# Attention's output through memory to feature rows: the division in two side steps, the projection without transposes

## The chip, the cores and the metric

The kernel runs on one core of a Trainium2 chip. A core has five engines that run side by side, each through its own instructions in order: TensorE (PE, matrix products, with its weight loads shown as PEld), VectorE (DVE), ScalarE (ACT), GpSimd (POOL) and SyncE (SP). Matrix products are written to PSUM, a small memory of banks; all else is held in SBUF, both with 128 partitions. Transfers between SBUF and the device's memory (DRAM) are issued by an engine's queue, mostly SP's here, and are moved by 16 DMA engines. An instruction that waits holds back all that stand behind it on its engine.

The metric is the device time of one execution in microseconds (us), the median of several runs.

## The reference

Two attentions and two MLPs on x of shape [2048, 256], in float32:

```
x = x + attn_a(layernorm(x))     # 16 query heads, 4 key/value heads, rotary angles, biases
x = x + ffn(layernorm(x))        # weights of 4 bits with scales, 2048 features, gelu(gate) * up
x = x + attn_b(layernorm(x))     # 16 heads, no biases
x = x + ffn(layernorm(x))        # the same weights again

# each attention, head size 16, causal:
scores = einsum('bthd,bshd->bhts', q, k) * 16 ** -0.5
probs  = softmax(where(causal, scores, -inf))
out    = einsum('bhts,bshd->bthd', probs, v).reshape(B, S, 256) @ Wo.T
```

## The kernel before

**Tiles.** The 2048 rows are four blocks of 512 (TB), block b in `xt[b]` as 128 partitions x 4 x 256. The 16 heads are four groups g of four. An attention is 16 *units* (b, g): 512 queries of one block against all keys up to them, for four heads. A unit has three parts.

- *Maxima* (`max_steps`): scores with queries on the partitions (L658, masks by L633 on the diagonal), and the maximum over the keys on DVE (L670, `mx`). `gather` brings the maxima together on DVE (L682 to L692), `turn` turns them on PE (L699) and ACT copies them to `mT` (L705).
- *Values* (`value_steps`): 4(b+1) key tiles, two `pair` steps each. PE subtracts the maximum (L747) and adds the scores with keys on the partitions (L752), ACT takes the exponential (L764, `e`), and PE multiplies by the values (L732) into `ps_av`. Each head has 32 partitions of `ps_av`: rows 0 to 15 are the output's features, row 16 (HD) is the sum of the exponentials, by a column of ones in the values.
- *The end* (`end`): ACT copies `ps_av` to `o` in SBUF (L779).

**From `o` to x.** `divide` transposes `o` in four 128x128 pieces on PE (L786), takes the reciprocal of the sums on DVE (L791) and multiplies into `att[b]` (L794), which has queries on the partitions and all 256 features along them. When the block's four groups are done, `out_steps` makes two halves of it: `turn` transposes `att` back to features on the partitions (L814, four a half) and ACT copies them to `aT` (L819); `project` multiplies by Wo (L826) and DVE adds to `xt[b]` (L831).

**The order.** All engines' orders are written by hand. In `run`, the value steps of unit n are the main list. Its side list holds the maxima of unit n+1 (8 steps per block of keys, and `gather`) and, spread among them by `blend`: the preparation of the next block (units with g = 0 and 1), the unpacking of the MLP's weights (first attention, from unit 4 on), and the `out_steps` of the block before (units with g = 0). `weave` runs, after each main step, as many side steps as are due, so that all are done two main steps ahead of the end. `divide` of the unit before stands first in the side list, so it comes after the first pair:

```
side = late + (blend(steps, more) if steps else more)
steps, end, divide = self.value_steps(b, g)
weave(steps, side, rest=2)
```

What is left of the last unit goes to the following MLP's first block, as side steps of its 16 `features` steps.

**Buffers and queues.** `ps_s` has three PSUM buffers, shared by the scores of both kinds and by the MLP; `ps_m` (transposes, projections, preparation) and `ps_av` have one each. SP issues nearly all transfers, in the order written: eight loads of queries `qT` for unit n+2 at the start of unit n (L619, three buffers), the stores of q and k as a high and a low part (L540, L544), the packed weights (L318), and the MLP's down weights `wd` (L907). POOL's queue loads `kT` (L606).

**The names that matter below:** L658/L670 scores and maxima, L747/L752/L764/L732 values, L779 `o`, L786/L791/L794 `divide`, L814/L819 `turn`, L826/L831 `project`, L619 `qT`.

Of the kernel before, what the change touches and what calls it, by code (L numbers as in the profile page):

```python
# [8 lines left out]
F32 = mybir.dt.float32  # L9
# [58 lines left out]
def tile_hybrid_layers(  # L68
# [326 lines left out]
    class Attention:  # L395
# [317 lines left out]
        def value_steps(self, b, g):  # L713

            nk = NT * (b + 1)
            held = {"pending": []}

            def values(half):

                self.settle()  # L720
                kt, q0, es_ = held["pending"][0]
                few = TB - q0 <= TB // 2
                if half == 1:
                    held["pending"].pop(0)
                    if few:
                        return
                elif kt == 0:
                    held["av"] = ps_av()
                own = slice(q0, TB) if few else slice(*((q0, TB // 2), (TB // 2, TB))[half])
                for j in range(4):  # L730
                    h = g if self.first else 4 * g + j
                    nc.tensor.matmul(  # L732
                        held["av"][32 * j : 32 * j + 32, own],
                        lhsT=self.vv[kt // NT][:, kt % NT, h * VW : h * VW + 32],
                        rhs=es_[j // 2][:, j % 2, own],
                        start=(kt == 0 and half == 0), stop=(kt == nk - 1),
                    )

            def pair(kt, p):
                q0 = max(0, kt - NT * b) * P  # L740
                diagonal = kt >= NT * b
                keys = slice((kt % NT) * P, (kt % NT + 1) * P)
                self.settle()
                pt = ps_s()

                for r in range(2):
                    nc.tensor.matmul(  # L747
                        pt[:, r, q0:], lhsT=sel[64 * r : 64 * r + 64, p, :],
                        rhs=self.mT[b, g][64 * r : 64 * r + 64, q0:], start=True, stop=False,
                    )  # L750
                for r in range(2):
                    nc.tensor.matmul(  # L752
                        pt[:, r, q0:], lhsT=self.key_rows(kt // NT, g, p, r, keys),
                        rhs=self.qT[b, g][64 * r : 64 * r + 64, p, q0:],
                        start=False, stop=not diagonal,
                    )
                e = self.wk.tile([P, 2, TB], F32, tag="e", name="e", bufs=4)

                def masked():
                    self.add_mask(pt, 1, q0)  # L760
                    exponentials()

                def exponentials():
                    nc.scalar.activation(e[:, :, q0:], pt[:, :, q0:], AF.Exp, scale=QK_SCALE)  # L764

                if diagonal:
                    self.owed.append(("exp", masked))
                else:
                    exponentials()
                if p == 0:  # L770
                    held["es"] = [e]
                else:
                    held["pending"].append((kt, q0, held["es"] + [e]))

            def end():
                values(0)
                values(1)
                o = pre.tile([P, TB], F32, tag="o", name="o")
                nc.scalar.copy(o, held["av"])  # L779
                held["o"] = o  # L780

            def divide():
                o = held["o"]
                pt = ps_m()
                for i in range(NT):
                    nc.tensor.transpose(  # L786
                        pt[:, i * P : (i + 1) * P], o[:, i * P : (i + 1) * P], ident
                    )
                heads = pt.rearrange("p (t j c) -> p t j c", t=NT, c=32)
                rec = small.tile([P, NT, 4], F32, tag="rec", name="rec")  # L790
                nc.vector.reciprocal(rec, heads[:, :, :, HD])  # L791
                if g == 0:
                    self.att[b] = pre.tile([P, NT, NG, 4, HD], F32, tag="att", name="att")
                nc.vector.tensor_tensor(  # L794
                    self.att[b][:, :, g], heads[:, :, :, :HD],
                    rec.unsqueeze(3).broadcast_to([P, NT, 4, HD]), ALU.mult,
                )

            steps = []
            for kt in range(nk):  # L800
                for p in range(2):
                    scored = lambda kt=kt, p=p: pair(kt, p)
                    steps.append((scored, lambda p=p: values(p)) if kt else scored)
            return steps, end, divide

        def out_steps(self, b):
            held = {}

            def turn(n):
                pt = ps_m()  # L810
                for i in range(2):
                    flat = self.att[b][:, 2 * n + i].rearrange("p g j c -> p (g j c)")
                    for c in range(2):
                        nc.tensor.transpose(  # L814
                            pt[:, (2 * i + c) * P : (2 * i + c + 1) * P],
                            flat[:, c * P : (c + 1) * P], ident,
                        )
                aT = pre.tile([P, 2, 2, P], F32, tag="aT", name="aT")
                nc.scalar.copy(aT, pt.rearrange("p (i c t) -> p i c t", i=2, c=2))  # L819
                held[n] = aT  # L820

            def project(n):
                po = ps_m()
                for i in range(2):
                    for c in range(2):
                        nc.tensor.matmul(  # L826
                            po[:, i * D : (i + 1) * D], lhsT=held[n][:, i, c, :],
                            rhs=self.wo[:, c, :], start=(c == 0), stop=(c == 1),
                        )
                to = xt[b][:, 2 * n : 2 * n + 2, :]  # L830
                nc.vector.tensor_tensor(  # L831
                    to, po.rearrange("p (i d) -> p i d", i=2), to, ALU.add
                )

            return [lambda n=n, f=f: f(n) for n in range(2) for f in (turn, project)]

        def run(self, extra, beside):

# [3 lines left out]
            late, ahead = [], []  # L842
            for n, (b, g) in enumerate(units):
                more = []
                if g == 0 and b > 0:
                    more += self.out_steps(b - 1)
                if g == 0 and b + 1 < NB:
                    ahead = self.prep_steps(b + 1)
                    few = -(-len(ahead) // 2)
# [8 lines left out]
                    steps, turn = self.max_steps(*units[n + 1])  # L858
                else:
                    more += beside  # L860
                side = late + (blend(steps, more) if steps else more)
                steps, end, divide = self.value_steps(b, g)
                weave(steps, side, rest=2)
                if turn:
                    turn()
                end()
                late = [divide]
            return late + [lambda: None] * 2 + self.out_steps(NB - 1)


    class Mlp:
# [183 lines left out]
```

## Time and profile before

The median is 1904.03 us of 3 runs (1902.41 to 1907.81). The profiled execution took 1904.93 us, its span from first to last instruction is 1903.1 us.

| | us | of the span |
|---|---|---|
| PE busy | 1772.5 | 93% |
| DVE busy | 1121.3 | 59% |
| ACT busy | 812.9 | 43% |
| POOL busy | 239.0 | 13% |
| L764, exponentials (ACT) | 573.4 | |
| L670, maxima (DVE) | 656.8 | |
| L786, transposes of `o` (PE) | 21.3 | |
| L814, transposes of `att` (PE) | 10.2 | |
| L826, projection (PE) | 31.7 | |
| L779, copies of `o` (ACT), 32 | 18.8 | |
| L819, copies `aT` (ACT), 16 | 9.2 | |
| DMA, mean rate | 34 GB/s | |

The first attention fills the stretch from about 71 to 651 us, the first MLP to 1028 us, the second attention to 1558 us, the second MLP the rest. Units of the second attention last from 12.3 us, (0,2), to 51.5 us, (3,0), counted from one copy of `o` to the next.

How to read the lines that follow: a group is line, engine, operation, what is written <- what is read, partitions x elements, count | busy us, mean ns of one | idle time of the engine just before, and who ended it. A timeline line is start in us, length in us, engine, line, operation, count, and in brackets the idle time before it. A wait line is who waited <- for whom: total us, times, longest us. A line of a stretch is from:to, length, then busy us and count of PE, PEld, DVE, ACT and POOL, the granted clock of PE, DMA's busy share and GB/s. DMA lines end with the median us from issue to landing.

### The profile page before, as it was taken

How to read it: one execution, taken by the hardware profiler on the slowest of the kernel's cores; microseconds unless marked ns; L12 is line 12 of the kernel's file. 1: busy time of each engine (PE TensorE's matmuls, PEld its weight loads, DVE VectorE, ACT ScalarE, POOL GpSimd, SP SyncE). 2: the span in 40 equal slices, each digit the busy share in tenths (PEclk: the TensorE clock that was granted, in tenths of full speed). 3: DMA queues.
4: the chain of work that ended last, by engine and by line, in shares of the span. 5: the costliest groups of instructions: out<-in, count | busy, mean ns of one | idle time of the engine just before them, and what ended most of it. 6: DMA issues, size and time to landing. Idle time of an engine off the chain costs nothing. (4 is left out here: it accounts for less than half of the span.)

```text
span 1903.1 us, 31836 instructions
## 1 busy us (share of the span) xinstructions
PE 1772.5 (93%) x13452; PEld 930.8 (49%) x13452; DVE 1121.3 (59%) x1676; ACT 812.9 (43%) x1069; POOL 239.0 (13%) x437
## 2 busy tenths in 40 slices
PE   5788889998999999999998899999899999999999
PEld 3344444344444446566555444444444444756656
DVE  4466587678788153535345667767877715363442
ACT  1334345465666631312223455555566663131221
POOL 4211311310010010111212010010000001011110
PEclk8879899999999999999999899999999999999999
DMA  4511310310101100000403241050000010000000
GB/s 105 118 46 34 73 26 26 72 41 24 34 24 35 45 6 1 0 1 20 102 1 80 56 83 41 12 95 19 23 7 7 2 46 1 11 1 11 7 6 12
DMA packets 42271, 64.24 MB, mean 34 GB/s; under 512 B 13840, under 2 KB 20880, under 8 KB 41872
## 3 DMA queue, kind: packets, MB, share of 16 engines
q1 hardware_dynamic: 33488, 45.93, 8.3%
q0 software_dynamic: 7680, 15.74, 5.0%
q8 instruction: 106, 1.74, 0.4%
q10 hardware_dynamic: 960, 0.52, 0.1%
q14 instruction: 37, 0.30, 0.1%
HBM read 44.24 MB, written 17.83 MB: 33 GB/s over the span
## 5 line engine op out<-in xcount | busy, mean ns | idle before, releaser
L764 ACT ACTIVATE e<-ps_s 128x1024 f32<-128x1024 f32 (+3 forms) x640 | 573.4, 897 | 433.7 <-PE ps_s L752 216.5
L670 DVE TENSOR_REDUCE mx<-ps_s 128x2 f32<-128x1024 f32 (+3 forms) x640 | 656.8, 1060 | 160.9 <-PE ps_s L633 93.2
L732 PE MATMUL ps_av<-e,v 128*32 128x256 f32 (+1 forms) x4608 | 370.6, 386 | 0.7 <-ACT e L764 0.7
L752 PE MATMUL ps_s<-qT,kT 64*128 64x512 f32 (+3 forms) x1280 | 341.9, 527 | 0.0
L658 PE MATMUL ps_s<-kT,qT 64*128 64x512 f32 (+3 forms) x1280 | 268.6, 428 | 45.4 <-DVE mx L670 20.1
L747 PE MATMUL ps_s<-mT,sel 64*128 64x512 bf16 (+3 forms) x1280 | 232.6, 357 | 36.7 <-DVE mx L670 21.4
L915 PE MATMUL ps_s<-xnT,wg 128*128 128x512 f32 x512 | 240.8, 593 | 0.0
L915 PE MATMUL ps_s<-xnT,wu 128*128 128x512 f32 x512 | 240.6, 592 | 0.0
L747 PEld LDWEIGHTS <-sel 64*128 64x128 bf16 x1280 | 77.1, 93 | 275.8 <-issue 269.4
L658 PEld LDWEIGHTS ps_s<-kT,qT 64*128 64x128 f32 x1280 | 125.7, 191 | 150.9 <-ACT e L764 66.9
L923 DVE TENSOR_TENSOR t<-ps_s,t 128x512 f32<-128x512 f32 x128 | 88.1, 689 | 166.4 <-POOL t L922 164.5
L921 ACT ACTIVATE t<-ps_s 128x512 f32<-128x512 f32 x128 | 76.2, 596 | 246.7 <-PE ps_s L915 246.3
L924 ACT ACTIVATE t<-t 128x512 f32<-128x512 f32 x128 | 80.6, 629 | 201.0 <-DVE t L923 201.0
L915 PEld LDWEIGHTS ps_s<-xnT,wu 128*128 128x128 f32 x512 | 97.3, 190 | 122.5 <-issue 122.5
L922 POOL TENSOR_SCALAR t<-t 128x512 f32<-128x512 f32 x128 | 79.3, 620 | 571.1 <-ACT t L921 570.6
L732 PEld LDWEIGHTS ps_av<-e,v 128*32 128x32 f32 x4608 | 97.0, 109 | 102.8 <-issue 79.8
L915 PEld LDWEIGHTS ps_s<-xnT,wg 128*128 128x128 f32 x512 | 95.3, 190 | 105.2 <-issue 103.5
L925 DVE SCALAR_TENSOR_TENSOR t<-t,ps_s 128x512 f32<-128x512 f32 x128 | 88.0, 688 | 89.0 <-ACT t L924 89.0
L752 PEld LDWEIGHTS ps_s<-qT,kT 64*128 64x128 f32 x1280 | 130.4, 198 | 0.0
L940 PE MATMUL ps_m<-wd,inter 128*128 128x256 f32 x512 | 114.5, 380 | 0.0
L940 PE MATMUL ps_av<-wd,inter 128*128 128x256 f32 x512 | 114.5, 380 | 0.0
L633 PE MATMUL ps_s<-mask_t,mask_w 64*128 64x64 bf16 x2048 | 108.4, 199 | 0.0
(125 smaller groups left out, 1171.5 us busy)
## 6 DMA issues: line engine op xcount, KB each, us to landing
qT<-h SPq DMA_DIRECT2D x256, 64.0 KB, 2.2
kT<-h POOLq DMA_DIRECT2D x96, 128.0 KB, 5.7
h<-high SPq DMA_DIRECT2D x24, 256.0 KB, 3.3
h<-low SPq DMA_DIRECT2D x24, 256.0 KB, 3.0
wd<-wd_kept SPq DMA_DIRECT2D x2, 2048.0 KB, 7.8
wd_kept<-dq_d SPq DMA_DIRECT2D x4, 512.0 KB, 2.7
out<-x SPq DMA_DIRECT2D x16, 128.0 KB, 1.7
x<-x SPq DMA_DIRECT2D x3, 512.0 KB, 5.2
```

What stands on the lines that cost most here:

```text
L633: nc.tensor.matmul(pt[:, r, to], lhsT=mask_w[rows, kind, part, :], rhs=mask_t[rows, kind, part, :], start=False, stop=(part == 1),)
L658: nc.tensor.matmul(pt[:, r, :w], lhsT=self.qT[b, g][64 * r : 64 * r + 64, p, i * P : (i + 1) * P], rhs=self.key_rows(c, g, p, r, slice(0, w)),
L670: nc.vector.tensor_reduce(held["mx"][:, i, 2 * p : 2 * p + 2, c], pt[:, :, :w], AX.X, ALU.max)
L732: nc.tensor.matmul(held["av"][32 * j : 32 * j + 32, own], lhsT=self.vv[kt // NT][:, kt % NT, h * VW : h * VW + 32], rhs=es_[j // 2][:, j % ...
L747: nc.tensor.matmul(pt[:, r, q0:], lhsT=sel[64 * r : 64 * r + 64, p, :], rhs=self.mT[b, g][64 * r : 64 * r + 64, q0:], start=True, stop=False,)
L752: nc.tensor.matmul(pt[:, r, q0:], lhsT=self.key_rows(kt // NT, g, p, r, keys), rhs=self.qT[b, g][64 * r : 64 * r + 64, p, q0:], start=Fals ...
L764: nc.scalar.activation(e[:, :, q0:], pt[:, :, q0:], AF.Exp, scale=QK_SCALE)
L915: nc.tensor.matmul(pt[:, k, :], lhsT=w[:, c, fc * P : (fc + 1) * P], rhs=self.xnT[b][:, c, :], start=(c == 0), stop=(c == 1),)
L923: nc.vector.tensor_tensor(t, gate, t, ALU.mult)
L924: nc.scalar.activation(t, t, AF.Tanh, scale=GELU_C)
L925: nc.vector.scalar_tensor_tensor(t, t, 1.0, gate, ALU.add, ALU.mult)
L940: nc.tensor.matmul(po[:, :D], lhsT=inter[:, fc, i * P : (i + 1) * P], rhs=wd[:, fc, :], start=(fc == 0), stop=(fc == NFC - 1),)
```

## The change

- `end` copies `ps_av` to `o` as before, then stores all of `o` to memory (`o_kept`, 256 KB). From there SP loads the four rows of sums into half of `den` ([128, 32]: four heads x 512 queries spread over 64 partitions), and the 64 feature rows into half of `att` (now [128 features, 512 queries]; two units, g even and odd, fill one). Three transfers a unit.
- After odd g there are two steps. `invert`: DVE takes the reciprocal of `den` (128x32), SP stores it (`rec_kept`) and loads it back with each head's row repeated over 16 partitions (`factor`, 128x512). `divide`: DVE multiplies `att` by `factor` in place, both in SBUF.
- `att` has features on the partitions already, so `out_steps` has no `turn`: `project` reads `att` as its weights.
- `late` isn't first in the side list any more: with part = length // (b + 1), `invert` is put at part // 2, `divide` at part + 1, and after g = 3 the two `project` at part + 4 and part + 6. Behind the last unit, pauses of three empty steps stand before `invert`, before `divide` and before the first `project`.

```diff
 def end():
     values(0)
     values(1)
     o = pre.tile([P, TB], F32, tag="o", name="o")
     nc.scalar.copy(o, held["av"])
-    held["o"] = o
+    kept = dram.tile([4, 32, TB], F32, tag="o", name="o_kept", bufs=2)
+    nc.sync.dma_start(out=kept.rearrange("j c t -> (j c) t"), in_=o)
+    if g % 2 == 0:
+        self.att[b, g // 2] = (
+            pre.tile([P, TB], F32, tag="att", name="att", bufs=2),
+            small.tile([P, 32], F32, tag="den", name="den"),
+        )
+    att, den = self.att[b, g // 2]
+    rows = slice(64 * (g % 2), 64 * (g % 2) + 64)
+    nc.sync.dma_start(
+        out=den[rows], in_=kept[:, HD].rearrange("j (s q) -> j s q", q=32)
+    )
+    nc.sync.dma_start(out=att[rows], in_=kept[:, :HD])
+
+def invert():
+    den = self.att[b, g // 2][1]
+    rec = small.tile([P, 32], F32, tag="rec", name="rec")
+    nc.vector.reciprocal(rec, den)
+    kept = dram.tile([8, TB], F32, tag="rec", name="rec_kept", bufs=2)
+    nc.sync.dma_start(
+        out=kept.rearrange("h (s q) -> (h s) q", q=32), in_=rec
+    )
+    factor = pre.tile([P, TB], F32, tag="factor", name="factor")
+    nc.sync.dma_start(
+        out=factor, in_=kept.unsqueeze(1).broadcast_to([8, HD, TB])
+    )
+    held["factor"] = factor
 
 def divide():
-    o = held["o"]
-    pt = ps_m()
-    for i in range(NT):
-        nc.tensor.transpose(
-            pt[:, i * P : (i + 1) * P], o[:, i * P : (i + 1) * P], ident
-        )
-    heads = pt.rearrange("p (t j c) -> p t j c", t=NT, c=32)
-    rec = small.tile([P, NT, 4], F32, tag="rec", name="rec")
-    nc.vector.reciprocal(rec, heads[:, :, :, HD])
-    if g == 0:
-        self.att[b] = pre.tile([P, NT, NG, 4, HD], F32, tag="att", name="att")
-    nc.vector.tensor_tensor(
-        self.att[b][:, :, g], heads[:, :, :, :HD],
-        rec.unsqueeze(3).broadcast_to([P, NT, 4, HD]), ALU.mult,
-    )
+    att = self.att[b, g // 2][0]
+    nc.vector.tensor_tensor(att, att, held["factor"], ALU.mult)
...
-            return steps, end, divide
+            return steps, end, [invert, divide] if g % 2 else []
 
 def out_steps(self, b):
-    held = {}
-    def turn(n):
-        pt = ps_m()
-        for i in range(2):
-            flat = self.att[b][:, 2 * n + i].rearrange("p g j c -> p (g j c)")
-            for c in range(2):
-                nc.tensor.transpose(
-                    pt[:, (2 * i + c) * P : (2 * i + c + 1) * P],
-                    flat[:, c * P : (c + 1) * P], ident,
-                )
-        aT = pre.tile([P, 2, 2, P], F32, tag="aT", name="aT")
-        nc.scalar.copy(aT, pt.rearrange("p (i c t) -> p i c t", i=2, c=2))
-        held[n] = aT
     def project(n):
         po = ps_m()
         for i in range(2):
+            t = (2 * n + i) * P
             for c in range(2):
                 nc.tensor.matmul(
-                    po[:, i * D : (i + 1) * D], lhsT=held[n][:, i, c, :],
+                    po[:, i * D : (i + 1) * D], lhsT=self.att[b, c][0][:, t : t + P],
                     rhs=self.wo[:, c, :], start=(c == 0), stop=(c == 1),
                 )
...
-    return [lambda n=n, f=f: f(n) for n in range(2) for f in (turn, project)]
+    return [lambda n=n: project(n) for n in range(2)]
 
 def run(self, extra, beside):
...
-        if g == 0 and b > 0:
-            more += self.out_steps(b - 1)
...
-        side = late + (blend(steps, more) if steps else more)
-        steps, end, divide = self.value_steps(b, g)
+        side = blend(steps, more) if steps else more
+        part = len(side) // (b + 1)
+        for at, step in zip((part // 2, part + 1, part + 4, part + 6), late):
+            side.insert(at, step)
+        steps, end, late = self.value_steps(b, g)
         weave(steps, side, rest=2)
         if turn:
             turn()
         end()
-        late = [divide]
-    return late + [lambda: None] * 2 + self.out_steps(NB - 1)
+        if g == NG - 1:
+            late += self.out_steps(b)
+    pause = [lambda: None] * 3
+    return pause + late[:1] + pause + late[1:2] + pause + late[2:]
```

## The prediction

> **What bounds the kernel now.** I read the busy table first, then the same counts by stage, the groups by form, TensorE's waits, the timeline of one unit boundary, and last the DMA issues. All is from one profiled execution: span 1903.1 us, 1904.93 us with what lies around it, 0.9 us above the median of 1904.03; I make the sum against it and subtract from the median.
>
> ```profile
> span 1903.1 us, 31836 instructions
> ...
> PE 1772.5 (93%) x13452; PEld 930.8 (49%) x13452; DVE 1121.3 (59%) x1676; ACT 812.9 (43%) x1069; POOL 239.0 (13%) x437
> ```
>
> ```profile
> 71.00:651.00 580.00, 525.17 (x5385) 248.38 (x5385) 398.51 (x583) 310.12 (x369) 92.29 (x160) 0.96 0.16 40
> 1052.00:1558.00 506.00, 475.24 (x5150) 227.22 (x5148) 349.12 (x442) 301.95 (x358) 19.36 (x35) 0.99 0.14 35
> ```
>
> These two stretches are the attentions (busy PE, PEld, DVE, ACT, POOL; clock; DMA share). PE is busy 91 and 94%, DVE 69%: PE sets the pace, DVE comes next, and DMA (0.14 to 0.16) is nearly free. What is removed or kept, on PE and then DVE:
>
> ```profile
> L826 PE MATMUL ps_m<-wo,aT 128*128 128x256 f32 x128 | 31.7, 390 | 7.4 <-ACT aT L819 7.3
> L786 PE MATMUL ps_m<-ident,o 128*128 128x128 f32 x128 | 21.3, 290 | 0.0
> L814 PE MATMUL ps_m<-ident,att 128*128 128x128 f32 x64 | 10.2, 281 | 3.1 <-DVE att L794 2.7 <-DVE x L831 0.4
> ```
>
> ```profile
> L794 DVE TENSOR_TENSOR att<-ps_m,rec 128x256 f32<-128x256 f32 x32 | 13.6, 424 | 1.1
> L791 DVE RECIPROCAL rec<-ps_m 128x16 f32<-128x16 f32 x32 | 8.2, 257 | 86.6 <-PE ps_m L786 86.6
> ```
>
> The last number is idle time before. DVE's 86.6 us hurts only as far as PE waits for DVE afterwards:
>
> ```profile
> PE ps_s L747 <- DVE mx L670: 21.4, 37, 1.2
> PE ps_s L658 <- DVE mx L670: 20.1, 44, 1.0
> ```
>
> One boundary, into unit (2,2) of the second attention, PE and then DVE; the copy of o (L779) ends at 1298.24, the zero T of my times below:
>
> ```profile
> 1298.29 0.65 PE L786 MATMUL ps_m<-ident,o 128*128 128x128 f32 x4
> 1298.87 0.50 PE L658 MATMUL ps_s<-kT,qT 64*128 64x512 f32 x2
> ...
> 1300.88 0.39 PE L747 MATMUL ps_s<-mT,sel 64*128 64x512 bf16 x2 [0.81 <-DVE mx L670]
> ```
>
> ```profile
> 1299.61 5.28 DVE L670 TENSOR_REDUCE mx<-ps_s 128x2 f32<-128x1024 f32 x5
> 1305.92 2.93 DVE L670 TENSOR_REDUCE mx<-ps_s 128x2 f32<-128x256 f32 x3 [1.02 <-PE ps_s L633]
> ```
>
> ```profile
> qT<-h SPq DMA_DIRECT2D x256, 64.0 KB, 2.2
> h<-high SPq DMA_DIRECT2D x24, 256.0 KB, 3.3
> wd_kept<-dq_d SPq DMA_DIRECT2D x4, 512.0 KB, 2.7
> out<-x SPq DMA_DIRECT2D x16, 128.0 KB, 1.7
> dq_s<-gate_s POOLq DMA_DIRECT2D x32, 32.0 KB, 2.1
> dq_q<-up_p SPq DMA_DIRECT2D x4, 256.0 KB, 3.1
> ```
>
> Last column: us from issue to landing. A chain of four such landings is what the change puts in place of the transposes.
>
> **Part 1, removed.** (a) 32 quartets of L786. By the timeline the next PE work starts 0.58 us after each (1298.29 to 1298.87); in the MLP, where two of them lie, I read 0.44. So 30 x 0.58 + 2 x 0.44 = 18.3 us of PE. Behind it DVE's reciprocal and product (0.68) delay the first maximum by about 0.2, which PE pays at 1300.88: up to 30 x 0.2 = 6 us more. (b) 16 quartets of L814: 12 x 0.55 + 4 x 0.44 = 8.4, plus PE's waits around them: 3.1 before L814, 7.3 for the ACT copy aT, 1.3 where a projection waits for ps_m behind att: 11.7. (c) 16 aT copies on ACT (9.2 us) and 21.8 us on DVE: no direct gain, ACT is idle half the time. Sum 38.4; bounds 27 (18.3 + 8.4, were every wait to return elsewhere) and 44. I take 40, near the top, since both waits vanish with their producers.
>
> **Part 2, added: when the steps become ready.** At each of 32 ends SP waits for the copy of o and issues o_kept, den, att; every second unit adds a reciprocal, rec_kept, factor and one product. 128 issues on SP, 0.46 apart (the eight qT issues take 3.66 us). SP mostly waits, so issue time costs nothing itself; order does. o_kept stands ahead of the eight qT loads of the unit after next. From T: o_kept lands at 2.8 (2.7 taken, between out<-x 1.7 and h<-high 3.3); den, 2.1 as the small load dq_s, at 5.0 (bounds 3.9 to 5.9); att is issued at 3.4, the qT loads until 7.6. Only then rec_kept: 2.0, landing at 9.7; then factor, 2.9 (wd_kept 2.7, dq_q 3.1), at 12.7 (bounds 11.8 to 13.5). In (3,2) no qT is loaded and factor is there at 10.9. The qT loads end 5.5 us later than now, and are first read a unit later; the shortest unit, (0,2), lasts 12.3 us against a landing at 9.8. Without that cover PE would lose the difference four times. The h stores behind them come 2 us later, with two high buffers and later units as cover. The 2 MB load of wd comes after the last att, 38 us or more before its first reader. POOL's queue is not passed.
>
> **Part 3, what waits.** By the new list of side steps, reciprocal stands behind 3 to 4 maxima and product behind 8. In (2,2) above the fourth maximum ends at T + 6.2 and the eighth at 1308.85, T + 10.6; both come 0.7 earlier without the transposes. So reciprocal finds den there (5.5 against 5.0), and product, at 9.9, waits 2.8 for factor. I placed the other units by the same count.
> - Reciprocal: (0,2) and (1,2) and (3,2) arrive at 4.0 to 4.9, the rest at 5 or later; waits add up to 3 us (bounds 0 and 11: den at 5.9 in ten units).
> - Product: arrivals in (1,2), (2,2), (3,0), (3,2) are 11.1, 10.9, 11.9, 9.3 in layer 1 and 9.4, 9.9, 10.9, 10.3 in layer 2: waits of 1.6, 1.8, 0.8, 1.6, 3.3, 2.8, 1.8, 0.6. The product itself is 0.69 (the 128x512 two-input rows). Queued behind it is the next maximum, whose ps_s buffer PE needs two allocations later; by the rows that leaves about 0.8, and DVE idles 2.1 to 2.7 there in three layer-1 units. Wait + 0.69 - 0.8 - idle gives PE losses of 0, 1.7, 0, 0, 2.5, 2.5, 1.7, 0.5: 9 us (bounds 2 and 24). In (0,2) only the next unit's maxima are behind it. In (1,0) and (2,0) it arrives at 15.6 or later; in the MLP at about 16.
> - First projection: three steps behind product, now with a wait on DVE: 1.8, 0.3, 1.2, 0.6, 0.8 in five units, 5 us (0 to 8).
> Costs 17; bounds 2 and 43. DVE's own work is unchanged within 6 us (21.8 out; 16 x 0.96 in).
>
> Sum: 1904 - 40 + 17 = 1881.
>
> One rule speaks against the change beyond this. The Trainium skill, "DMA: Bandwidth & Descriptors", section "Why a DMA increments its semaphore by 16 and not by 1", says a transfer uses only as many of the 16 engines as divide the outermost dimension on both sides: 4 for den and att, 8 for factor. No DMA of this trace has so small an outer dimension. With the page's 436 GB/s for 16 engines I estimate factor at 3.2 us rather than 2.9; by that the sum would be 1883.
>
> **The rivals.**
> - *All hidden.* The landings take the lower bounds and DVE's earlier start pays: 44 - 2 saved, 1862. For it: 0.14 DMA share; against it: rec_kept stands behind eight qT issues.
> - *Not on the path.* The 81 waits of PE on maxima (41.5 us) show that the ps_s loop with DVE sets the pace in part. If quartets' 26.7 us return as such waits, 40 - 27 - 17 leaves 1908, and half of it 1894; I put this case at 1901. Against it: PE 94% busy, and the boundary stall follows the scores, which move up.
> - *DVE held by the round trip (slower).* Place: reciprocal and product in the ten units with g = 2 or (3,0). Each us more on every landing brings den 2 us later and factor about 1 more beyond that: 3 us x 10 = 30 us. Break-even is 23/30 = 0.8 us per landing; at 1.5 more (the loads of down_p take 4.7, those of kT 5.7) the time is 1881 + 45 = 1926. For it: DVE runs in order and a full maximum takes 1.22 of each 1.45 us step, so a held DVE can hardly catch up. Against it: the queue is quiet after boundaries, and 64 KB loads land in 2.2.
>
> **Numbers.** Main case 0.53 (1866 to 1898 for itself), all hidden 0.16, not on the path 0.14, DVE held 0.17. A measurement here tells 0.3%, 5.7 us. Faster 0.53 + 0.16 + 0.05 of the third = 0.74; same 0.08; slower 0.18 with a tail of the third. Range: 1858 (44 saved, the rest the run-to-run spread) to 1911 (38 saved, 43 paid, short of the far slow tail).
>
> **What would show it.** Right: PE's work about 30 us less, its waits for aT gone, DVE's 86.6 us before the reciprocal replaced by waits on den of 0 to 2 us and on factor of 1 to 3 us in (1,2), (2,2), (3,0), (3,2), none in (1,0), (2,0); factor landing near T + 12.7. Wrong: den after T + 7 or factor after T + 16, DVE then in front of PE for each; or units whose length is unchanged though the quartets are gone.

## The result, and the profile after

The changed kernel takes 1973.32 us (median of 4 runs, 1957.55 to 1974.77) against 1904.62 us before (4 runs, 1902.41 to 1907.81): 1.0352 times as long, 95% interval 1.0325 to 1.0379. The forecast was 1881 us, in a range that ended at 1911. It was wrong by 92 us and in sign. (Ratios, here and below, are of undisturbed runs; of e5's four runs one, of 2447.55 us at a granted clock of 0.65, is left out of its ratio.)

The profiled execution took 1974.77 us. Its page gives the span and the busy times, and the table by stretches the two attentions (from:to, length, busy us of PE, PEld, DVE, ACT, POOL, the granted clock, DMA's share, GB/s):

```profile
span 1973.0 us, 31681 instructions
...
PE 1775.2 (90%) x13260; PEld 924.4 (47%) x13260; DVE 1114.9 (57%) x1644; ACT 804.1 (41%) x1053; POOL 239.5 (12%) x437
```

```profile
73.00:697.00 624.00, 525.19 (x5302) 244.07 (x5299) 395.09 (x567) 306.17 (x363) 92.46 (x160) 0.92 0.19 50
1104.00:1626.00 522.00, 471.82 (x5054) 223.51 (x5050) 346.75 (x428) 297.67 (x351) 19.34 (x35) 0.97 0.18 44
```

The first attention grew by 44 us (580 to 624), the second by 16 (506 to 522) and by another 4 in its unit (0,1), which lies before this stretch. PE has 192 instructions fewer and yet 2.7 us more busy time, at a granted clock of 0.955 where it was 0.978; its idle time grew from 130.6 us (1903.1 - 1772.5) to 197.8. What PE waits for, in the list of waits after (us, times, longest):

```profile
PE ps_s L747 <- DVE mx L670: 49.2, 47, 7.9
PE ps_s L658 <- DVE mx L670: 31.2, 43, 4.6
```

Before, these two lines had 21.4 and 20.1 us, and none was longer than 1.2. PE waits 39 us more for maxima. DVE does no more work (1114.9 us), so DVE itself must be waiting. Its groups after, whose last columns are the idle time before them and who ended it:

```profile
L813 DVE TENSOR_TENSOR att<-att,factor 128x512 f32<-128x512 f32 x16 | 11.1, 691 | 47.0 <-DMA factor<-rec_kept 34.4 <-issue 12.5
...
L799 DVE RECIPROCAL rec<-den 128x32 f32<-128x32 f32 x16 | 5.5, 346 | 8.2 <-DMA den<-o_kept 8.2
...
L343 DVE TENSOR_SCALAR dq_t<-dq_b 128x128 uint32<-128x128 uint32 x24 | 5.2, 218 | 52.1 <-POOL dq_b L332 52.1
```

The first two are the waits that the prediction spoke of: 3 us on `den` and 14 on `factor` forecast, 8.2 and 47.0 found. The third it did not name at all. L343 unpacks the MLP's weights, which the change does not touch; before, DVE waited 3.2 us there. The three add up to 107 us.

Where the third comes from is seen at the end of unit (0,3) of the first attention. SP's own queue, after (start, length, how many):

```profile
144.19 0.34 SPq L783 DMA_DIRECT2D o_kept<-o  x1
147.92 0.54 SPq L791 DMA_DIRECT2D den<-o_kept  x1
148.51 0.53 SPq L794 DMA_DIRECT2D att<-o_kept  x1
149.13 5.60 SPq L619 DMA_DIRECT2D qT<-h  x8
154.82 0.37 SPq L318 DMA_DIRECT2D dq_q<-gate_p  x1
160.68 0.34 SPq L802 DMA_DIRECT2D rec_kept<-rec  x1
162.12 0.60 SPq L806 DMA_DIRECT2D factor<-rec_kept  x1
```

and before:

```profile
140.00 3.57 SPq L619 DMA_DIRECT2D qT<-h  x8
143.66 0.37 SPq L318 DMA_DIRECT2D dq_q<-gate_p  x1
```

`dq_q`, the packed weights, stands on SP behind the eight `qT` loads. Before, all nine went out around the end of the unit, `dq_q` 2.0 us after the copy of `o` (T). Now `o_kept`, the wait for its landing, `den` and `att` stand ahead, and `dq_q` goes out at T + 10.7. What hangs on it, two engines further on, in the timeline after (in brackets the idle time before):

```profile
157.52 0.61 POOL L332 COPY dq_b<-dq_q 128x512 uint8<-128x512 uint8 x1 [52.39 <-DMA dq_q<-gate_p]
158.17 0.23 DVE L343 TENSOR_SCALAR dq_t<-dq_b 128x128 uint32<-128x128 uint32 x1 [10.97 <-POOL dq_b L332]
...
159.85 0.61 PE L747 MATMUL ps_s<-mT,sel 64*128 64x512 bf16 x2 [7.85 <-DVE mx L670]
```

POOL was waiting for the load, DVE stands 10.97 us for POOL with maxima queued behind, and PE stands 7.85 us for a maximum. The unpacking is spread over the first attention from (1,0) on, and that attention lost most.

The boundary that the prediction worked through is the one into unit (2,2) of the second attention, T at 1360.90. SP and then DVE:

```profile
1360.93 0.32 SPq L783 DMA_DIRECT2D o_kept<-o  x1
1364.83 0.54 SPq L791 DMA_DIRECT2D den<-o_kept  x1
1365.42 0.52 SPq L794 DMA_DIRECT2D att<-o_kept  x1
1366.05 5.71 SPq L619 DMA_DIRECT2D qT<-h  x8
1371.86 0.37 SPq L802 DMA_DIRECT2D rec_kept<-rec  x1
1373.66 0.60 SPq L806 DMA_DIRECT2D factor<-rec_kept  x1
```

```profile
1366.95 0.35 DVE L799 RECIPROCAL rec<-den 128x32 f32<-128x32 f32 x1 [1.04 <-DMA den<-o_kept]
...
1377.28 0.69 DVE L813 TENSOR_TENSOR att<-att,factor 128x512 f32<-128x512 f32 x1 [5.76 <-DMA factor<-rec_kept]
```

The reciprocal is done at T + 6.4, but `rec_kept` goes out at T + 11.0, after the last `qT`. `factor` goes out at T + 12.8 and its product starts at T + 16.4. The eight `qT` loads take 5.71 us to issue, not 3.66. SP's waits after show why:

```profile
SPq L791 <- DMA o_kept<-o: 64.9, 32, 4.4
SPq L619 <- DMA att<-o_kept: 43.7, 22, 4.4
```

At 22 of the boundaries the last of the eight waits for `att` to land, which was issued eight transfers earlier: some 2 us each time.

The units, from one copy of `o` to the next in us (e1 to e4 are experiments below):

| unit | before | after | e1 | e2 | e3 | e4 |
|---|---|---|---|---|---|---|
| first attention (1,0) | 37.9 | 47.9 | 42.6 | 48.2 | 36.5 | 38.9 |
| (1,1) | 46.9 | 55.7 | 45.1 | 50.3 | 46.0 | 47.1 |
| (2,0) | 47.2 | 52.7 | 47.4 | 53.8 | 44.0 | 44.8 |
| (2,1) | 51.7 | 56.3 | 48.3 | 55.7 | 48.3 | 49.9 |
| second attention (1,2) | 23.9 | 30.9 | 31.6 | 23.7 | 23.8 | 23.9 |
| (2,2) | 35.2 | 41.5 | 40.8 | 35.0 | 34.9 | 35.3 |

Units without such waits gained little: (2,1), (2,3) and (3,1) of the second attention 1.2, 0.9 and 0.3 us, (3,3) nothing.

### The profile page after: what moved, and what is told of

Its sections match the earlier page's. It is cut to its first block, busy times and chain, and to the rows that moved or that the text cites. A ratio compares the mean times of both kernels' runs of the same rounds, so it can differ in the third digit from the quotient of the medians.

```text
span 1973.0 us, 31681 instructions
## 1 busy us (share of the span) xinstructions
PE 1775.2 (90%) x13260; PEld 924.4 (47%) x13260; DVE 1114.9 (57%) x1644; ACT 804.1 (41%) x1053; POOL 239.5 (12%) x437
## 5 line engine op out<-in xcount | busy, mean ns | idle before, releaser
L732 PE MATMUL ps_av<-e,v 128*32 128x256 f32 (+1 forms) x4608 | 375.4, 390 | 1.5 <-ACT e L764 1.5
L752 PE MATMUL ps_s<-qT,kT 64*128 64x512 f32 (+3 forms) x1280 | 349.1, 538 | 0.0
L658 PE MATMUL ps_s<-kT,qT 64*128 64x512 f32 (+3 forms) x1280 | 273.1, 434 | 61.2 <-DVE mx L670 31.2
L747 PE MATMUL ps_s<-mT,sel 64*128 64x512 bf16 (+3 forms) x1280 | 236.8, 363 | 77.9 <-DVE mx L670 49.2
L747 PEld LDWEIGHTS <-sel 64*128 64x128 bf16 x1280 | 77.2, 93 | 322.8 <-issue 317.7
L658 PEld LDWEIGHTS ps_s<-kT,qT 64*128 64x128 f32 x1280 | 132.6, 195 | 172.8 <-DVE mx L670 71.2
L732 PEld LDWEIGHTS ps_av<-e,v 128*32 128x32 f32 x4608 | 97.5, 109 | 106.2 <-issue 81.6
```

The costliest lines, as they stand in the source:

```text
L658: nc.tensor.matmul(pt[:, r, :w], lhsT=self.qT[b, g][64 * r : 64 * r + 64, p, i * P : (i + 1) * P], rhs=self.key_rows(c, g, p, r, slice(0, w)),
L732: nc.tensor.matmul(held["av"][32 * j : 32 * j + 32, own], lhsT=self.vv[kt // NT][:, kt % NT, h * VW : h * VW + 32], rhs=es_[j // 2][:, j % ...
L747: nc.tensor.matmul(pt[:, r, q0:], lhsT=sel[64 * r : 64 * r + 64, p, :], rhs=self.mT[b, g][64 * r : 64 * r + 64, q0:], start=True, stop=False,)
L752: nc.tensor.matmul(pt[:, r, q0:], lhsT=self.key_rows(kt // NT, g, p, r, keys), rhs=self.qT[b, g][64 * r : 64 * r + 64, p, q0:], start=Fals ...
```

## The experiments

### One wait taken away, the other, both

Two causes are on the table. The *queue theory*: the packed weights' loads come late on SP, 52 us of DVE's waiting. The *factor theory*: the round trip of the sums comes after its product's place in DVE's order, 47 us. A third, that the transfers as such slow the core or its clock, would leave both edits with little effect.

e1 issues the packed weights' loads from POOL's queue, where POOL is their reader anyway; the round trip stays as it is.

```diff
 def load(...):                       # L318, both forms of it
-    nc.sync.dma_start(out=q, in_=src)
+    nc.gpsimd.dma_start(out=q, in_=src)
```

> The changed kernel with one edit: the loads of the packed weights (dq_q, twelve in the first attention) are issued on GpSimd's queue instead of SP's, so they no longer stand behind o_kept, den, att and the qT loads. Theory Q (the round trip holds SP's queue, the packed weights come late, VectorE waits 52 us for GpSimd's first unpacking step): these waits fall back to about 3 us, units (1,0), (1,1), (2,0), (2,1) and (1,2) of the first attention get about 32 us back, the second attention stays as it is; 1973 falls to about 1941. Theory F (VectorE held by den and factor is what costs): no more than 8 us, above 1960.

Measured: 1938.93 us, 1.0166 [1.0131, 1.0200] of before. DVE's waits in e1:

```profile
DVE att L813 <- DMA factor<-rec_kept: 50.2, 12, 6.8
...
DVE dq_t L343 <- POOL dq_b L332: 1.2, 1, 1.2
```

The weights' wait is gone, the factor's is larger (57.0 us before L813 in all, 47.0 in the changed kernel), and nearly half of the loss is gone, as the queue theory had it.

e2 leaves the loads on SP and puts the four late steps further back in the side list, so that `factor` has time.

```diff
-for at, step in zip((part // 2, part + 1, part + 4, part + 6), late):
+own = (3, 4, 6, 8) if (b, g) == (1, 0) else (3, 9, 12, 14)
+for at, step in zip((part // 2 + own[0], *(part + x for x in own[1:])), late):
     side.insert(at, step)
```

> The changed kernel with the reciprocal three side steps later, the product eight later and the projections behind it (three to four later in unit (1,0), where a preparation step would be split otherwise). Theory F: VectorE's waits for den and factor (55 us) go to under 10, units (1,2), (2,2) of both attentions and (3,0) of the first get about 27 us back: about 1946. Theory Q: the units with late packed weights keep their loss of 32 us, so no better than 1940. If the waits for factor were covered already: 1973.

Measured: 1938.41 us, 1.0182 [1.0160, 1.0204], 34.9 us less, where the factor theory expected 27. Its waits of DVE are the other way about:

```profile
DVE dq_t L343 <- POOL dq_b L332: 53.4, 7, 10.3
...
DVE att L813 <- DMA factor<-rec_kept: 11.8, 3, 6.2
```

e3 has both edits.

> Both edits, the packed weights on GpSimd's queue and the later steps. If Q and F together are the whole loss and the removed transposes are worth what was forecast (40 us), this comes to 1870 to 1885, below the kernel before. If the transposes are worth little, the sum of both edits alone gives 1973 - 32 - 27 = 1914. If a third cause is left, above 1920. The share of time with a halved clock falls to that of before (0.978) in the first two cases.

Measured: 1891.46 us, 0.9939 [0.9916, 0.9962]: faster than before, between the 1870 to 1885 of a full gain and the 1914 of a small one.

```profile
DVE att L813 <- DMA factor<-rec_kept: 9.8, 3, 5.1
```

So the two waits are the loss: 81.9 us (1973.32 - 1891.46) go with them. Each alone gives back 34 to 35 us, less than half of 81.9; in (1,0), by the table, neither alone brings the unit near its old length and both do. The two causes are about equally large. The table shows where each sits: e1 mends most of the first attention and leaves (1,2) and (2,2) of the second as they were, e2 the reverse. A third cause, the transfers as such, is left little: e3 has them all, and stands 7.5 us above the next version, which has none.

### What the removed work was worth

e4 keeps the changed structure, with reciprocal, product and projection at their new places, but without any of the five transfers. It leaves out the division by the right sums and the placing of the features: reciprocal and product read `o` itself.

```diff
-# o_kept, den, att, rec_kept, factor: all five transfers
+held["o"] = o
-nc.vector.reciprocal(rec, den)
+nc.vector.reciprocal(rec, held["o"][:, :32])
-nc.vector.tensor_tensor(att, att, held["factor"], ALU.mult)
+nc.vector.tensor_tensor(att, held["o"], held["o"], ALU.mult)
```

> The changed kernel with no transfer at all in the division: o_kept, den, att, rec_kept and factor are left out; the reciprocal reads a piece of o, the product multiplies o by itself into att, so the division and the placing of the features are left out and the attention's output is other numbers. It prices the removed transposes and copies without the round trip. Forecast: 40 us saved against before, 1864. If the removed TensorE time comes back as waits for maxima: 1890 to 1900. If above 1904, TensorE was not what these steps held.

Measured: 1884.00 us, 0.9891 [0.9870, 0.9911], between its two theories (1864; 1890 to 1900). Without any round trip the change gives 20 us, not the 40 that the prediction's first part counted. PE is busy 1744.3 us, 28.2 less than before, as forecast (26.7). But PE idles 7.5 us more, 138.1. Its waits in e4:

```profile
PE ps_s L658 <- DVE mx L670: 19.1, 40, 1.1
PE ps_s L747 <- DVE mx L670: 18.6, 39, 0.7
PE ps_s L747 <- ACT e L764: 17.5, 33, 0.9
PE ps_s L658 <- ACT e L764: 14.3, 26, 2.2
...
PE ps_m L882 <- ACT xnT L883: 7.0, 4, 2.3
```

With a small one at L732, PE's waits for maxima fell from 41.5 us before to 37.7, and those for exponentials rose from 18.0 to 33.3; and 7.0 us appear in the MLP that were 0.2. The 11.7 us of waits around the transposes did vanish, and more than that came back as waits for ACT.

One more wait grew in e4: DVE stands 11.1 us at L343, where it was 3.2 before.

```profile
DVE dq_t L343 <- POOL dq_b L332: 11.1, 5, 3.1
```

After (1,0), for one, the load goes out at T + 2.0 as before, but DVE comes to L343 0.7 us earlier. At the 0.85 us per us of waiting that the runs below give, about 7 of the missing 20 us may lie here. This is an estimate: no run has e4 with these loads on POOL's queue.

Does the order bring on the waits for ACT? With `late` no longer first in the side list, the first maxima come right after the first pair. e9 puts an empty step first in e4's side list, so that a pair of values stands where the transposes stood.

```diff
+side = [lambda: None] + side
 weave(steps, side, rest=2)
```

> The version without any transfer, with one empty step put first in every unit's side list, where the division's step stood before the change, so that one score and not two follows the first pair. Theory B (half of the gain is lost at the boundary, where two scores in a row fill the three ps_s buffers and TensorE waits 0.6 us twice for maxima): the boundary waits shrink and the time falls from 1884 by 8 to 16 us, to 1868 to 1876. If the maxima set the pace there whatever the order: 1881 to 1887.

Measured: 1880.57 us, 0.9885 [0.9859, 0.9911], which is not to be told from e4.

```profile
PE ps_s L658 <- ACT e L764: 21.6, 41, 2.2
PE ps_s L658 <- DVE mx L670: 20.1, 45, 1.1
PE ps_s L747 <- DVE mx L670: 13.9, 28, 1.1
```

In place of L747 it is L658 that waits for exponentials, and the waits for maxima and exponentials come to 62.2 us, 8.8 less than in e4. The time followed by 3.4 us at most, and does not reach the 1868 to 1876 of this theory. So the order of the first steps is not what holds most of the gain back; what does, these two runs do not show beyond the waits above.

### The transfers, their order, and the slow one

e5 is the kernel before with the three transfers of each `end` added, into tiles that nobody reads. Nothing waits for the round trip; only what stands behind on SP can suffer.

```diff
 nc.scalar.copy(o, held["av"])
 ...                                  # kept, den and spare are made
+nc.sync.dma_start(out=kept.rearrange("j c t -> (j c) t"), in_=o)
+nc.sync.dma_start(out=den[rows], in_=kept[:, HD].rearrange("j (s q) -> j s q", q=32))
+nc.sync.dma_start(out=spare[rows], in_=kept[:, :HD])      # never read
```

> The kernel before, with o_kept, den and att added at every unit's end on SP's queue and never read; transposes, division and projection stay as before, and no engine waits for the new data. Theory Q (the queue held by the round trip is a cause by itself): VectorE's waits for GpSimd's first unpacking step rise from 3 to about 45 us, the first attention's units (1,0) to (2,1) lose about 30 us with the halved clock, the second attention loses under 3: 1935. If only waits on the new data cost: 1904 to 1908.

Measured: 1924.35 us, 1.0113 [1.0095, 1.0130].

```profile
DVE dq_t L343 <- POOL dq_b L332: 28.8, 6, 7.9
```

The loss sits where the weights are unpacked: the six units (1,0) to (2,1) of the first attention lost 17.4 us together, and the second attention 0.2. The mechanism was as expected, the size smaller (28.8 us of waits where 45 were expected). The clock, 0.980, did not fall.

e7 changes the order on SP alone: the eight `qT` loads go out at the end of the unit, ahead of `o_kept`, instead of behind `att`.

```diff
-if n + 2 < len(units):
-    self.load_q(*units[n + 2])          # at the unit's start
+if n == 0:
+    self.load_q(*units[2])
 ...
 weave(steps, side, rest=2)
+if n + 3 < len(units):
+    self.load_q(*units[n + 3])
 if turn:
     turn()
 end()
```

> The changed kernel with one order swapped: the eight qT loads of the next unit but one are issued before the copy of o and its three transfers, not behind them; no queue or step is moved otherwise. Theory W (each us that VectorE is held costs about 0.85 us, whatever holds it): the packed weights are issued at about T + 5.3 instead of 10.7, factor lands near T + 12.3 instead of 16, den 2 us later; VectorE's waits fall from 107 to about 62 us and the time to about 1935. If the order of these loads does not matter: 1973. If later den costs more than the rest gains: above 1960.

Measured: 1943.30 us, 1.0209 [1.0186, 1.0233], less of a gain than the 1935 expected.

```profile
DVE dq_t L343 <- POOL dq_b L332: 38.4, 6, 9.9
...
DVE rec L799 <- DMA den<-o_kept: 20.7, 9, 4.2
...
DVE att L813 <- DMA factor<-rec_kept: 13.0, 9, 2.8
```

With 4.8 us more at L813, 77 us of waits are left of 107 (62 were expected). With `qT` out of its way `factor` comes earlier; `den` now waits behind `qT`, and the packed weights still stand behind the landing of `o_kept`. No order of one queue serves both.

e11 is the changed kernel with `att` loaded in four parts of 16 rows, so that no load has four as its outermost size.

```diff
-nc.sync.dma_start(out=att[rows], in_=kept[:, :HD])
+for j in range(4):
+    at = 64 * (g % 2) + HD * j
+    nc.sync.dma_start(out=att[at : at + HD], in_=kept[j, :HD])
```

> The changed kernel with the load of att cut into four loads of 16 rows each (one head). Now att's 128 KB land so late that the eighth qT load, which stands eight transfers behind, is issued 5.5 us after att where issue alone takes 3.7. If att is slow because its outermost dimension of four keeps it on four of the sixteen DMA engines: the loads of 16 rows land within 3 us and SP's waits for att (44 us) go to under 5. If it is slow for another reason, the waits stay. The time moves little, 1965 to 1978, as three more issues take what the waits took.

Measured: 1966.09 us (two runs), 1.0335 [1.0306, 1.0365]. SP's wait for `att` fell from 43.7 us to

```profile
SPq L619 <- DMA att<-o_kept: 1.5, 4, 0.7
```

and the eight `qT` loads after (0,3) take 3.63 us again, not 5.60. So the wait was `att`'s own slow landing. Little of it reaches DVE, because the four issues take 1.84 us instead of 0.53: from `den`'s issue to `dq_q`'s it is 6.3 us instead of 6.9. DVE's three waits still come to 106.5 us, and the 7 us in time can't be told from nothing: the changed kernel's own runs span 17 us, and the two ratios' intervals overlap.

Why `att` lands slowly shows in the trace's single packets. Each transfer ends with packets of 4 bytes, which I read as one end mark per engine: 16 for `o_kept` and `dq_q`, 4 for `att` and `den`, 8 for `factor`. `o_kept` moves its 256 KB in 0.8 us where nothing disturbs it. `att` takes 2.05 us for 128 KB at the end of (3,2) of the second attention, with no `qT` load behind it. `factor` takes 1.6 to 1.8 us for 256 KB and is through 3.0 to 3.2 us after its issue. `dq_q`, a load of the same size in packets of the same size, is through after 2.3 (the one at 154.82). So the fewer marks, the slower, at equal size.

### What a held DVE costs, and whether the clock adds to it

PE's busy time in the changed kernel is 30.9 us above e4's, for the same instructions at a lower clock. The *clock theory* says that a wait of DVE costs more than itself, since PE is throttled after it stands. e6a adds to the kernel before a piece of DVE work of 8.8 us, read by nobody, in six units of the second attention (b > 0, g even), after six side steps; e6b one of 3.25 us at the same places.

```diff
+if not self.first and b > 0 and g % 2 == 0:
+    def hold():
+        z = self.wk.tile([P, TB], F32, tag="z", name="z", bufs=1)
+        nc.vector.memset(z, 0.0)
+        for _ in range(12):                   # e6b: 4
+            nc.vector.tensor_tensor(z, z, z, ALU.add)
+    side.insert(6, hold)
```

> The kernel before, with VectorE held for about 8.6 us (12 additions of 128x512 on a scratch tile) once in each of six units of the second attention ((1,0), (1,2), (2,0), (2,2), (3,0), (3,2)), as one wait of the changed kernel holds it. Theory C (a long hold empties TensorE, its granted clock then halves for some microseconds, and the loss is larger than the hold): half-clock spells of 3.4 to 7 us after each hold, 60 us or more lost in all, 1964 or more. Without theory C: six times the hold less about 1.5 us of cover, 43 us, 1947, and no new half-clock spells.

> The same with holds of 4 additions, about 3 us each, the size of the waits that the forecast allowed for. Theory C: too short to halve the clock, so 6 x (3 - 1.5) = 9 us, 1913, no new half-clock spells. If any stall halves the clock: 25 us or more. If VectorE has more cover than thought: under 1907.

Measured: e6a 1953.16 us, 1.0265 [1.0251, 1.0278]; e6b 1914.54 us, 1.0062 [1.0049, 1.0075]. One hold of e6a, and the stretches around it (the clock is the third number from the end):

```profile
1517.32 8.69 DVE L868 TENSOR_TENSOR z<-z 128x512 f32<-128x512 f32 x12
```

```profile
1506.00:1516.00 10.00, 9.13 (x104) 4.36 (x98) 7.07 (x13) 7.03 (x10) 0.00 (x0) 1.00 0.01 2
1516.00:1526.00 10.00, 4.34 (x54) 2.00 (x51) 9.54 (x15) 3.44 (x4) 0.00 (x0) 0.79 0.00 0
1526.00:1536.00 10.00, 8.81 (x64) 3.45 (x63) 6.96 (x9) 4.53 (x5) 0.00 (x0) 0.69 0.00 0
```

The clock does fall, to 0.79 and 0.69, and in the last stretch PE does 64 matmuls in 8.81 us of busy time; in the first it did 104 in 9.13. And yet the second attention, in which all holds lie, took 580.4 us where it took 530.4 before: 50.0 us more for 52.8 us of holds, 47.0 of them in the six units. The clock theory as put, 60 us or more, falls.

That the clock adds nothing is not shown, though. With e6b's holds, 19.5 us in all, the second attention lost 12.7 us. So the further 33.3 us of hold cost 37.3 (38.6 by the medians of all runs). If the 6.8 us that e6b's holds did not cost are taken off e6a's too, 46.0 us would be expected, and 4 of the 50.0 may be the clock's. This is an estimate and no more, since single units without a hold differ by up to 2.4 us between these runs. But behind the hold above DVE is not catching up all the time: it waits for PE, 0.89 us here and 1.18 and 0.61 at the next maxima, while the clock is low.

```profile
1528.69 1.23 DVE L670 TENSOR_REDUCE mx<-ps_s 128x2 f32<-128x1024 f32 x1 [0.89 <-PE ps_s L658]
```

Nor is the small hold free of it, against what was expected: behind one of e6b, at 1487.56, PE waited 1.85 us for a maximum, and the clock fell in the same stretch.

```profile
1486.00:1496.00 10.00, 8.00 (x78) 3.41 (x70) 7.36 (x10) 4.70 (x5) 0.00 (x0) 0.83 0.00 0
```

Over the whole run this can't be seen: 0.979 for e6b, 0.969 for e6a, 0.978 before. In sum, a us of hold cost 0.65 us in e6b and 0.95 in e6a, clock included.

The Trainium skill, "TensorE: Matmul & The Clock Gate", section "HAM oscillation — how this bites in real kernels", describes matmuls that run at half rate after a wait of over 3.4 us, and counts what the half rate costs as a loss beside the wait. The rows above show the throttling, here also after a wait of 1.85 us, and leave room for a loss beside the waits of some 4 us over six holds.

### Can the change be made to pay further?

e3 has three waits on `factor` left, the longest 5.1 us. e8 is e3 with the product of the first pair of block 0 moved from unit (0,2), the shortest, into (0,3).

```diff
+if (b, g) == (0, 2):
+    late, kept_back = late[:1], late[1:]
+if (b, g) == (0, 3):
+    side.insert(2, kept_back[0])
```

> The version with both edits (packed weights on GpSimd's queue, later steps), and the product of the first block's first pair of units moved from unit (0,2) to the start of (0,3), since (0,2) lasts 11 us only and the factor comes after 13. There VectorE still waited 10 us for factor, and units (0,3) and (0,1) of the second attention were 4 us longer than before. Expected: the waits for factor under 2 us, units (0,3) 3 to 4 us shorter, 1884 to 1888, against 1891.5; the floor is the run without transfers, 1884.

Measured (6 runs): 1888.89 us, 0.9930 [0.9910, 0.9949], just above the 1884 to 1888 expected and not to be told from e3. In the second attention unit (0,3) is 4.5 us shorter, as expected; in the first it is not. The waits left on `factor`, with 2.0 us more at L813:

```profile
DVE att L813 <- DMA factor<-rec_kept: 2.3, 2, 2.1
```

e10 is e8 with e9's empty first step.

> The best version so far (packed weights on GpSimd's queue, later steps, the first product moved to unit (0,3)), with the same empty step first in every side list. Theory B: from 1889 to about 1877. Without it: 1886 to 1892.

Measured (6 runs): 1887.80 us, 0.9921 [0.9899, 0.9942], the same as e8; its theory had 1877. These are the best versions that compute the whole reference: 14 to 16 us faster than before. They stand 4 us above e4, and the intervals overlap; but e4, with its 11.1 us at L343, is no floor for them, since their loads go by POOL's queue. No run moves these loads alone in the kernel before, where DVE waits 3.2 us for them, so that about 3 us of the gain may be the loads' and not the change's.

One line sums the runs up. With e3 and the changed kernel as its two ends (11.0 and 107.2 us of DVE waits on packed weights, `den` and `factor`; 1891.46 and 1973.32 us), a us of waiting costs 0.85. The others, by that line and measured: e1 (68.1 us) 1940 and 1938.9; e2 (65.2) 1938 and 1938.4; e7 (76.9) 1948 and 1943.3; e11 (106.5) 1973 and 1966.1; e8 (5.5) 1887 and 1888.9. It is 7 us off at e11, and within 5 elsewhere.

## Why the prediction was wrong

**What failed first: the list of what stands behind the new wait.** Part 2 said "SP mostly waits, so issue time costs nothing itself; order does", and then went through `qT`, the h stores and the load of wd. The packed weights' loads (L318) stand on the same queue, in the same place, and were not in the list, although the prediction's own table of transfers had a row for them (`dq_q<-up_p`, 4 issues of 256 KB). Their reader is POOL, and POOL's reader is DVE, in order, with the maxima behind. This is 52.1 us of waiting where 3.2 were; with e2 it stands nearly alone, and costs 47 us (1938.41 - 1891.46). The forecast had nothing for it.

**What failed second: when `factor` lands.** Forecast T + 12.7, bounds 11.8 to 13.5; found T + 16.4 in (2,2), and product starts between T + 13.2 and T + 17.8 in most of the tight units. The terms, in (2,2):
- `o_kept` landed late: `den` was issued at T + 3.9, not 2.8. At 22 of 32 boundaries it was T + 2.0 to 2.1, earlier than I took; at seven it was 2.9 to 4.8.
- The eight `qT` loads took 5.71 us, not 3.66: 2.05 more, the wait for `att`.
- `rec_kept` went as forecast, 1.8 us from its issue to that of `factor` (2.0 taken).
- `factor` took 3.6 us from issue to product, not 2.9.

Product came to its place at T + 10.6 (9.9 forecast), so the wait was 5.76 us, not 2.8. Over all units 47.0 us, not 14.3: 32.4 in the eight units that had the 14.3, and 14.5 in four that had none. These are (0,2) of both attentions (4.1 and 3.6) and (1,0) and (2,0) of the second (3.5 and 3.4), where the product was placed at T + 15.6 or later and came to its turn at T + 11.2 and 11.1. With e1 this wait stands nearly alone and costs 47 us (1938.93 - 1891.46); the forecast had 9 us, and 5 in the projection. (Its list of PE losses has 2.5 twice where its own rule gives 3.2 and 2.7, 0.9 us too little, which changes nothing.)

**The slow transfers.** The Trainium skill, "DMA: Bandwidth & Descriptors", section "Why a DMA increments its semaphore by 16 and not by 1", holds that a transfer uses only as many engines, up to 16, as divide its outermost size on both sides: four for `att` and `den`, eight for `factor`. The prediction let it change one landing, by 0.3 us. The runs agree with it: in four parts of 16 rows `att` lands in time for the queue (43.7 us of SP's waits become 1.5), and `factor` takes 1.6 to 1.8 us of packets where `o_kept`, as large, takes 0.8. In (2,2) `factor`'s last packet is through 3.16 us after its issue, near the estimate by the page (3.2); the product starts 0.46 later. What the prediction missed is who waits for the slow transfer: the queue itself, eight issues later.

**What failed third: the size of the gain.** Part 1 took 40 us, near its upper bound of 44, "since both waits vanish with their producers". PE's work fell as forecast (28.2 us in e4). The waits around the transposes vanished too, and came back at the exponentials and in the MLP; e4 shows 20 us, below the lower bound of 27. The rival *Not on the path* named this return, expecting it on the maxima, and of the 26.7 us of PE work; it came on the exponentials, and took the 11.7 us of waits and a quarter of the work (7.5 of 28.2). How much of this is due to DVE's 7.9 us more at L343 in e4 is not settled.

**What held.** PE stands because DVE stands in front of `factor`, in (1,2) and (2,2) of the second attention above all, as Part 3 laid out; its cover of 0.8 us a wait lies between the 0.5 of e6a's holds and the 1.1 of e6b's, and its rule that the rest is lost one for one is near (1.12 between the two sizes). The reciprocal's waits, 8.2 us, lie within its bounds of 0 to 11. The rival *DVE held by the round trip* is the mechanism of one half: its break-even of 0.8 us more per landing was passed, and with e1, where only this half is at work, the time is 1938.9 against its 1926. Its chance of 0.17 looks too low: the time of every landing was taken from transfers that nothing blocked. "Factor after T + 16" was named as what would show the forecast wrong, and (2,2) shows it.

In the prediction's terms the sum is 1904.3 - 20.3 (e4) + 7.5 (from e4 to e3) + 81.9 (both waits) = 1973.4. The terms are differences of these very runs, so that it comes out proves nothing; it shows their sizes.

**Why `o_kept` was late.** Here too the packets tell. At the boundary into (2,2), 15 of the 16 end marks of `o_kept` came by 1.63 us after its issue, as at the quick boundaries, and the last at 3.41. In that time, from 0.86 to 2.42, one packet of 16 KB of the queue that the profile calls "q8 instruction" was under way. The same stands at the ends of (0,3) and (1,1) of the first attention and of (1,1) of the second; at none of the 22 quick boundaries was there such a packet. That it held up one of the 16 engines is inferred, since the trace names no engine of a packet. Which boundaries it met is chance, as far as the runs show. At the other three slow ones loads of `kT`, `qT` or `factor` were under way.

**Open.** Why a us of waiting costs 0.85 in this kernel, and 0.65 and 0.95 in e6b and e6a; what the clock's share in it is; and what ACT would have to do earlier for the rest of PE's saved work to count.

## What to carry to other kernels

When a transfer that waits is put on a queue, write down every transfer behind it in the issue order of that queue, and for each its reader and the reader's reader: here the dearest wait lay two engines away, in work that the change never touched. Here a round trip through memory was only as fast as what stood in its queue let it be, so its consumer belongs as far back in an in-order engine's list as the data allow, and unrelated loads on another queue; these two edits turned 3.5% slower into 0.6% faster. Work removed from the busiest engine is worth what the next engines in its loop let through, here 20 of 28 us of work and none of the 11.7 us of waits, as far as e4 shows it.

## What was unexpected in the hardware

- A load of 64 rows written as 4 x 16 holds SP's queue up at the eighth transfer behind it, 2 us each time (43.7 us over 22 boundaries); as four loads of 16 rows it does not (1.5 us).
- The granted clock fell to 0.79 and 0.69 in the 10 us stretches during and after a hold of 8.8 us, and to 0.83 around one of 3.25 us, after a wait of PE of 1.85 us. Even so, six holds of 8.8 us lengthened their attention by 50.0 us, less than their own 52.8.
- The same store of 256 KB (`o_kept`) lets the next transfer go 2.0 us after the copy at one boundary and up to 4.8 us after it at another. At four boundaries 15 of its 16 end marks came on time and one 1.6 to 2.2 us later, after a 16 KB packet of the instruction queue.
- 256 KB took 0.8 us of packets as `o_kept` (16 end marks) and 1.6 to 1.8 as `factor` (8); 128 KB as `att` (4) took 2.05 or more.
